# Two convolution layers in one kernel: the order of two half convolutions and a gelu in layer 0, and where layer 1's first pixel sums are kept

## The chip, the cores and the metric

The kernel runs on one core of one Trainium2 chip. A core has five engines that run side by side, each in its own program order: TensorE (PE in the profile, with PEld for the loads of its weights) multiplies matrices into PSUM; VectorE (DVE), ScalarE (ACT) and GpSimd (POOL) work on tiles; SyncE (SP) issues the DMAs between the main memory and the on-chip memory. They wait for each other by semaphores. The metric is the device time of one execution in microseconds (us), the median of several runs.

## The reference

The input x has 4 batches of 64 channels of 256 x 256 pixels, in fp32. Layer 0 and layer 1 each add their result to their input. Cut to what matters:

```python
# layer 0, on h0 = groupnorm(x)
h = gelu(conv3x3(h0, c1_w) + c1_b)               # 64 -> 64 channels
xa, k = split(conv1x1(h, c2_w))                  # 64 -> 128 channels, in halves
xs = gelu(taps_3x1(taps_1x3(xa)))                # depthwise, 3 taps across and 3 down
w = top2(softmax(mean(xs) @ gate_w.T))           # per batch: needs all of xs
out = xs + sum_i w_i * e_i_w3(e_i_w2(k) * e_i_w1(xs))   # three experts of rank 2, 4 and 8
x = x + proj(out)
# layer 1, on y = groupnorm(x)
h = relu(batchnorm(conv3x3(y, quantized(w1)) + b1))     # statistics over all batches
h = batchnorm(conv3x3(h, quantized(w2)) + b2)
x = x + relu(h + y)
```

## The kernel before

Two image rows lie on the 128 partitions at once (64 channels each). An *octet* is 8 rows of one batch, 32 to a batch; a *chunk* is 16 rows, 16 to a batch.

Layer 0 is worked octet by octet. Its 3x3 convolution takes two neighbouring pixels together by four products (0 to 3), whose inputs are sums and differences of pixels that POOL writes into v_ring (front_v, L492). Products 1 and 2 go into one PSUM bank (tag c, two buffers) by front_conv_a and front_conv_b with (1, 2). front_butterfly then brings them into the form in which products 0 and 3 can be added: ACT copies half (m, L558), DVE adds and subtracts (L559, L560). front_conv_a and front_conv_b with (0, 3) add the others, and front_h (two gelus on ACT, L566) empties the bank into h. The taps follow: front_taps_a and front_taps_b on PE (tag a, one buffer), front_taps_h with L615 on ACT, L616, L619 and L622 on DVE and the gelu L633 on ACT. front_k (L643), front_q (L681), front_proj (L653 on, with the DVE add L667) and the experts' out_slot (L754 on PE, L762 and two bn_stats L764 on DVE) share tag p, one buffer. divide sets a tick on POOL (L442) between two phases of PE: POOL's memset waits for the last matmul before it, and the first matmul of the next front_conv_b or front_taps_b waits for the memset.

The order is written out by hand: plan is a table from (step, order) to calls, and at(step, order, call) adds to it. Each octet takes one step in layer 0, so there are 128 steps, 32 to a batch. In step g, by order number: front_conv_a of octet g with (1, 2) at 1; out_slot of the batch before at 2; front_conv_a of octet g-1 with (0, 3) at 3; front_k, in one step of four, at 3.5; front_taps_a of octet g-3 at 4; divide at 5; front_proj of g-4 at 6; front_conv_b of g with (1, 2) at 7 and its butterfly at 7.5; front_conv_b of g-1 with (0, 3) at 8 and its gelu at 8.5; front_taps_b of g-3 at 9; front_q, in one step of four, at 10; front_taps_h at 11. The program order of PE, SP, DVE and POOL is that of the table; that of ACT too from step 124 on, and before that a scheduler sets it. Group norm's statistics of the next batch (L394 on DVE) are spread over the steps of batches 0 to 2. Experts of a batch run from step 36 on, one batch late: out_load and low_load (L738 and L744) fetch y and ranks, out_slot computes, and stores y_d<-y (L771) go out after each chunk.

At step 128 (CONV1) layer 1 begins; the tail of layer 0 is stretched to every second step (place). A chunk y_in is loaded (conv1_load, L788), normalized (conv1_affine, L793 on ACT) and split into a high and a low part (conv1_split: L354 on ACT, L356 on DVE and POOL). Sums of neighbouring pixels are made by add_pixels (L364 on POOL) and split as well (conv1_sums: L370 on ACT, L372 on POOL). conv1_a and conv1_b then work 8 rows (one d) in two steps: products into ps_h (tag c) and, from the sums, ps_hm (tag c while d < 4 in batch 0, then tag a). leave empties them: L335 on ACT writes m (tag ranks while d < 4 in batch 0), L336 on DVE writes h. In batch 0 the sums of the first four chunks were kept in tag t (one buffer, that of front_taps_h) and in tags xs or ranks. The last batch's experts run under layer 1, from step 164 on, a slot every 4.6 steps. conv2 works in the same manner, and a last pass adds everything up.

Of the kernel before, what the change touches and what calls it, by code (L numbers as in the profile page):

```python
# [9 lines left out]
F32 = mybir.dt.float32  # L10
# [7 lines left out]
B, C, H, W = 4, 64, 256, 256  # L18
P = 128
# [28 lines left out]
GF = GP * W  # L48
NG = NPAIR // GP
NOCT = NG // 2  # L50
CG = 4
CPAIR = CG * GP
# [11 lines left out]
def conv_preact_kernel(ctx: ExitStack, tc: tile.TileContext, io, col128, colset, col64):  # L64
# [30 lines left out]
    def flat(t):  # L95
        return t.rearrange("p a b -> p (a b)")
# [14 lines left out]
    def half_tile(pool, name, bufs, dtype=F32R):  # L111
        return pool.tile([P, CPAIR + 1, PW], dtype, tag="half", name=name, bufs=bufs)

    HW = W // 2
# [11 lines left out]
    def sum_tiles(pool, name, bufs):  # L126

        t = flat(half_tile(pool, f"sum_{name}", bufs))[:, 0 : 2 * (CPAIR + 1) * HW]
        t = t.rearrange("p (u a b) -> p u a b", u=2, b=HW)
        return [t[:, u] for u in range(2)]  # L130
# [4 lines left out]
    def split_tiles(pool, name):  # L135

        return [half_pads([half_tile(pool, f"half_{name}{i}{j}", 6) for j in range(2)]) for i in range(2)]
# [4 lines left out]
    work = layers.enter_context(tc.tile_pool(name="work", bufs=2))  # L142

    def chunk_out(name, tag, bufs):
        return work.tile([P, CPAIR, W], F32, tag=tag, name=name, bufs=bufs)
# [16 lines left out]
    def at(step, order, call, *args):  # L162
        plan[step, order].append((call, args))
# [181 lines left out]
    CUTS = (0, 5), (5, CPAIR + 1)  # L345

    def split(tiles, y, engines, cuts=CUTS):

        parts = []
        for a, e in cuts:  # L350
            upper, lower = (by_pixels(t, a, e) for t in tiles)
            parts.append((upper, lower, y[:, a:e, :].rearrange("p a (j e) -> p a e j", e=2)))
        for upper, _, y in parts:
            nc.scalar.activation(upper, y, AF.Copy)  # L354
        for (upper, lower, y), engine in zip(parts, engines):
            engine.tensor_tensor(lower, y, upper.bitcast(F32), ALU.subtract)  # L356

    def add_pixels(y, name, places, size):

        sums = []  # L360
        for (a, e), (pool, tag, bufs) in zip(CUTS, places):
            t = pool.tile(size, F32, tag=tag, name=f"s_{name}_{a}", bufs=bufs)
            t = (flat(t) if len(size) > 2 else t)[:, 0 : (e - a) * HW].rearrange("p (a b) -> p a b", b=HW)
            nc.gpsimd.tensor_tensor(t, y[:, a:e, 0::2], y[:, a:e, 1::2], ALU.add)  # L364
            sums.append(t)
        return sums

    def split_sums(tiles, sums):
        for (a, e), t in zip(CUTS, sums):
            nc.scalar.activation(tiles[0][:, a:e, :], t, AF.Copy)  # L370
        for (a, e), t in zip(CUTS, sums):
            nc.gpsimd.tensor_tensor(tiles[1][:, a:e, :], t, tiles[0][:, a:e, :].bitcast(F32), ALU.subtract)  # L372
# [403 lines left out]
    def out_end(b):  # L776
        gn2[b] = const.tile([P, 3], F32, name=f"gn2_{b}")
        yield from group_norm(st_y.pop(b), c128("avg4"), gn2[b][:, 0:2], f"y{b}")
        nc.vector.tensor_scalar(gn2[b][:, 2:3], gn2[b][:, 0:1], gn2[b][:, 1:2], -1.0, ALU.mult, ALU.mult)


    y_in, h_out, st_h = {}, {}, {}
# [16 lines left out]
    def conv1_split(b, k):  # L799

        split(halves[k % 2], y_in[b, k], (nc.vector, nc.vector if b == B - 1 else nc.gpsimd))

    sums_in = {}

    def conv1_add(b, k):
        sums_in[b, k] = add_pixels(y_in[b, k], f"1_{b}_{k}", [(work, "xs", 4)] * 2, [P, 2, GF])

    def conv1_prepare(b, k):

        places = (work, "t", 1), ((work, "ranks", 2) if k == 2 else (work, "xs", 4))  # L810
        sums_in[b, k] = add_pixels(y_in[b, k], f"1_{b}_{k}", places, [P, 2, GF])
        conv1_split(b, k)
        conv1_sums(b, k)

    def conv1_sums(b, k):
        del y_in[b, k]
        split_sums(sums[k % 2], sums_in.pop((b, k)))
# [75 lines left out]
    def at_each(places, chain):  # L893

        for place in places:
            at(*place, next, chain, None)
# [8 lines left out]
    def plan_front(b):  # L905
        t = b * F_STEPS
        place = tail if b == B - 1 else (lambda step: step)
        for k in range(NCH):
            if b > 0 or k >= 2:
                for call in (front_alloc, front_pad, front_load):  # L910
                    at(max(t + 2 * k - 3, 0), 0, call, b, k)
        for n in range(NOCT):
            g = t + n
            at(g, 1, front_conv_a, b, n, (1, 2))
            at(place(g + 1), 3, front_conv_a, b, n, (0, 3))
            at(place(g + 3), 4, front_taps_a, b, n)
            at(g, 5, divide)
            for step in (g + 1, g + 3):
                if step >= CONV1:
                    at(place(step), 5, divide)  # L920
            at(place(g + 4), 6, front_proj, b, n)
            at(g, 7, front_conv_b, b, n, (1, 2))
            at(g, 7.5, front_butterfly, b, n)
            at(place(g + 1), 8, front_conv_b, b, n, (0, 3))
            at(place(g + 1), 8.5, front_h, b, n)

            for half, before in ((1, 1), (0, 2)):
                if b > 0 or n > before - 1:
                    at(g - before, 5.4, front_v, b, n, half, ((1, 2),))
                    at(g - before, 9 if half else 9.5, front_v, b, n, half, ((0, 3),))  # L930
            at(place(g + 3), 9, front_taps_b, b, n)
            at(place(g + 3), 11, front_taps_h, b, n)
        for j in range(NOCT // 4):
            at(place(t + 4 * j + 5), 3.5, front_k, b, j)
            at(place(t + 4 * j + 7), 10, front_q, b, j)
        e = place(t + NOCT + 3)
        at_each(((e, 2.5), (e, 5.7), (e, 8.7)) if e < CONV1 else ((e + 1, 12.7), (e + 3, 12.7), (e + 5, 12.7)), gate(b))

# [12 lines left out]
    def plan_out(b, steps, order, end):  # L951

        for k in range(NCH):
            for call in (low_load, out_load):
                at(steps[2 * k - 3] if k > 1 else steps[0] - 2, order + 0.2, call, b, k)
            for i in range(2):
                at(steps[2 * k + i], order, out_slot, b, k, i)
        at_each(end, out_end(b))

    conv1_pool, halves, sums = [], [], []  # L960
# [13 lines left out]
    def plan_conv1(b):  # L974
        t = CONV1 + b * (NG + 1)
        if b == 0:
            at(t - 4, -1, conv1_first)
            at(t, 12, conv1_open)
        for k in range(NCH):
            load, affine, ready = t + 4 * k - 11, t + 4 * k - 6, t + 4 * k - 4  # L980
            if b == 0 and k < 4:

                load, affine, ready = ((t - 4, t - 3, t - 2), (t - 1, t, t + 2), (t + 1, t + 3, t + 4), (t + 5, t + 7, t + 8))[k]
            at(max(load, t + 6) if b == 0 and k > 3 else load, 0, conv1_load, b, k)
            at(affine, 5.6 if affine < t else 12.2, conv1_affine, b, k)
            if b == 0 and k < 4:

                at(ready, 5.6 if k < 2 else 13.1, conv1_prepare, b, k)
            else:
                at(affine, 12.3, conv1_add, b, k)  # L990
                at(ready, 13.1, conv1_split, b, k)
                at(ready, 13.2, conv1_sums, b, k)
        for d in range(NG // 2):
            at(t + 2 * d, 13, conv1_a, b, d)
            at(t + 2 * d + 1, 13, conv1_b, b, d)
        at(t + NG, 13, conv1_end, b)

    for b in range(B):
        plan_front(b)
        if b < B - 1:  # L1000
            plan_stats(b + 1, b * F_STEPS + 1, 2.7)
            t = (b + 1) * F_STEPS + 4
            e = t + NOCT + 1
            steps, end = [t + n for n in range(NOCT)], ((e, 5.5), (e + 1, 5.5), (e + 1, 9.95), (e + 2, 5.5))
# [5 lines left out]
        else:  # L1010
            t, e = CONV1 + 36, CONV1 + b * (NG + 1) - 10
# [25 lines left out]
    h_in = {}  # L1037
# [17 lines left out]
        split(halves2[i % 2], h_in[i], (nc.vector, nc.vector), cuts)  # L1055

    def conv2_add(i):
        sums_in[i] = add_pixels(h_in[i], f"2_{i}", [(halves_pool, "s", 2)] * 2, [P, 5 * HW])

    def conv2_sums(i):  # L1060
        del h_in[i]
# [10 lines left out]
    halves_pool = halves_stack.enter_context(tc.tile_pool(name="halves2", bufs=1, reuse_waits="tile"))  # L1072
    halves2 = split_tiles(halves_pool, "2")
    sums2 = [sum_tiles(halves_pool, f"2{i}", 6) for i in range(2)]
    h2, st_h2 = {}, {}

    def chunk_h2(b, k):
# [27 lines left out]
    with tc.manual_schedule(  # L1105
# [15 lines left out]
        for d in range(2 * len(chunks)):  # L1121
            i = d // 2
# [13 lines left out]
    steps = chunks[-KEEP:] + chunks[:-KEEP]  # L1136
# [21 lines left out]
    for i, (b, k) in enumerate(steps):  # L1158
        if i + AHEAD < len(steps):
            end_load(i + AHEAD)  # L1160
        y, h = y_of.pop(i), h2.pop((b, k))
# [7 lines left out]
        j = i - 3 + KEEP  # L1169
# [115 lines left out]
```

## Time and profile before

| what | us |
|---|---|
| median of 3 runs (lowest to highest) | 3377.47 (3375.42 to 3378.84) |
| the profiled execution, its own time | 3377.74 |
| its span, first to last instruction | 3376.0 |
| PE busy | 2683.1 (79%) |
| DVE busy | 2679.1 (79%) |
| ACT busy | 1658.2 (49%) |
| POOL busy | 1606.3 (48%) |

By stage (from the windows of the profile; us busy):

| stage | window | PE | DVE | ACT | POOL |
|---|---|---|---|---|---|
| start, statistics of batch 0 | 0 to 120 | 50.8 | 82.7 | 17.6 | 36.2 |
| layer 0, about one batch | 120 to 480 | 334.7 | 241.7 | 153.1 | 166.5 |
| layer 0, about one batch | 480 to 850 | 349.1 | 298.1 | 145.1 | 157.1 |
| layer 0, about one batch | 850 to 1220 | 348.6 | 295.0 | 146.7 | 156.3 |
| layer 0's last batch and the seam | 1220 to 1590 | 331.6 | 248.0 | 153.9 | 149.7 |
| layer 1, first convolution | 1590 to 2300 | 670.1 | 639.6 | 456.0 | 505.8 |
| layer 1, second convolution | 2300 to 2700 | 398.2 | 383.2 | 307.1 | 295.4 |
| end of it and last pass | 2700 to 3376 | 200.1 | 490.8 | 278.7 | 139.3 |

A stage whose PE column is close to the window's length is bound by PE. The profile's name for a line such as "PE ps_c L449 <- POOL v_ring L492" reads: PE stood idle before a matmul of line 449 into ps_c, and of the things that it waited for POOL's write of v_ring at line 492 was seen last. Matmul ends are modelled, so gaps of a tenth of a microsecond on PE mean nothing.

### The profile page before, as it was taken

How to read it: one execution, taken by the hardware profiler on the slowest of the kernel's cores; microseconds unless marked ns; L12 is line 12 of the kernel's file. 1: busy time of each engine (PE TensorE's matmuls, PEld its weight loads, DVE VectorE, ACT ScalarE, POOL GpSimd, SP SyncE). 2: the span in 40 equal slices, each digit the busy share in tenths (PEclk: the TensorE clock that was granted, in tenths of full speed). 3: DMA queues.
4: the chain of work that ended last, by engine and by line, in shares of the span. 5: the costliest groups of instructions: out<-in, count | busy, mean ns of one | idle time of the engine just before them, and what ended most of it. 6: DMA issues, size and time to landing. Idle time of an engine off the chain costs nothing.

```text
span 3376.0 us, 60519 instructions
## 1 busy us (share of the span) xinstructions
PE 2683.1 (79%) x24832; PEld 1772.7 (53%) x24832; DVE 2679.1 (79%) x2810; ACT 1658.2 (49%) x1799; POOL 1606.3 (48%) x1833
## 2 busy tenths in 40 slices
PE   2999999999999999997899999998999999300000
PEld 1555555554545555544667777776877878200000
DVE  7666588878888776665899998998999999866666
ACT  0344433343433343344666666667777777422222
POOL 2444543443444444443678777666777777100000
PEclk9999999999999999998999999999999999755555
DMA  8565588778886767674688987564666664599999
GB/s 305 161 174 137 143 263 270 229 218 251 268 267 191 206 196 218 197 216 144 219 291 283 303 298 246 218 252 173 238 238 238 238 232 171 202 412 412 412 412 387
DMA packets 356453, 838.27 MB, mean 248 GB/s; under 512 B 22288, under 2 KB 284944, under 8 KB 293456
## 3 DMA queue, kind: packets, MB, share of 16 engines
q1 hardware_dynamic: 356176, 834.40, 74.0%
q8 instruction: 195, 3.19, 0.4%
q14 instruction: 82, 0.67, 0.1%
HBM read 493.00 MB, written 341.31 MB: 247 GB/s over the span
## 4 chain that ended last, share of the span: by engine, by line
PE 58%; DVE 14%; DMA 12%; POOL 7%; issue 4%; ACT 4%; SPq 3%; POOLq 0%; ACTq 0%; DVEq 0%
PE ps_h L310 23%; PE ps_c L449 14%; DMA y_end<-y_d 10%; PE ps_a L449 7%; POOL v_ring L492 5%; PE ps_h2m L310 3%; PE ps_o L754 3%; PE ps_hm L310 2%; PE ps_p L449 2%; DVE half L356 2%; PE ps_k L643 2%; PE ps_q L681 2%; DVE h L336 2%; DVE y L762 1%; DVE t L619 1%
## 5 line engine op out<-in xcount | busy, mean ns | idle before, releaser
L310 PE MATMUL ps_h<-half,w_q 128*128 128x512 f32 x4096 | 1033.4, 404 | 23.4 <-DVE h L336 16.9
L310 PEld LDWEIGHTS ps_h<-half,w_q 128*128 128x128 f32 x4096 | 778.2, 191 | 253.0 <-issue 27.4
L372 POOL TENSOR_TENSOR sum<-s,sum 128x640 fp32r<-128x640 f32 (+1 forms) x256 | 556.8, 2196 | 195.0 <-ACT sum L370 189.3
L492 POOL TENSOR_TENSOR v_ring<-x 128x256 f32<-128x256 f32 x1024 | 593.3, 617 | 61.4 <-DMA x<-in_x 47.2
L449 PE MATMUL ps_c<-v_ring,u 64*64 64x256 f32 (+1 forms) x6472 | 391.3, 372 | 74.9 <-POOL v_ring L492 63.4
L449 PEld LDWEIGHTS ps_c<-v_ring,u 64*64 64x64 f32 x6472 | 273.6, 134 | 283.2 <-POOL v_ring L492 157.9
L442 POOL MEMSET tick<- 128x1 f32 x132 | 13.1, 99 | 820.1 <-PE ps_a L449 811.2
L336 DVE SCALAR_TENSOR_TENSOR h<-ps_h,scale_w,m 128x1024 f32<-128x1024 f32 x256 | 326.9, 1277 | 88.7 <-ACT m L335 88.7
L449 PE MATMUL ps_a<-h,av 64*64 64x512 f32 (+1 forms) x3568 | 386.3, 534 | 10.4 <-DVE t L619 9.1
L449 PE MATMUL ps_c<-v_ring,c1s 64*64 64x256 f32 (+1 forms) x6472 | 387.3, 368 | 0.5 <-DVE ps_c L560 0.5
L633 ACT ACTIVATE xs<-t 128x1024 f32<-128x1024 f32 x128 | 135.3, 1057 | 411.4 <-DVE t L622 375.9
L449 PEld LDWEIGHTS ps_c<-v_ring,c1s 64*64 64x64 f32 x6472 | 267.9, 133 | 129.0 <-DVE t L616 47.8
L1163 ACT ACTIVATE v<-y_end,shift,gn 128x2048 f32<-128x2048 f32 x64 | 133.8, 2092 | 321.2 <-DMA y_end<-y_d 314.4
L667 DVE TENSOR_TENSOR x<-ps_p,x 128x1024 f32<-128x1024 f32 x128 | 156.2, 1220 | 157.1 <-PE ps_p L449 131.5
L1164 DVE SCALAR_TENSOR_TENSOR h<-h,ss,v 128x2048 f32<-128x2048 f32 x64 | 150.2, 2351 | 160.3 <-DMA h<-h_d 103.4
L558 ACT ACTIVATE m<-ps_c 128x512 f32<-128x512 f32 x128 | 76.6, 598 | 378.3 <-PE ps_c L449 371.3
L356 DVE TENSOR_TENSOR half<-h,half 128x1280 fp32r<-128x1280 f32 (+1 forms) x128 | 254.4, 2029 | 7.7 <-ACT half L354 7.7
L616 DVE SCALAR_TENSOR_TENSOR t<-ps_a,m,t 128x1020 f32<-128x1020 f32 x128 | 163.5, 1277 | 122.2 <-ACT t L615 122.2
L449 PEld LDWEIGHTS ps_a<-h,av 64*64 64x64 f32 x3568 | 161.9, 133 | 148.5 <-issue 112.5
L356 DVE TENSOR_TENSOR half<-yn,half 128x1280 fp32r<-128x1280 f32 x80 | 211.3, 2658 | 4.2 <-ACT half L354 4.2
L335 ACT ACTIVATE m<-ps_hm,m,scale_w 128x512 f32<-128x512 f32 x128 | 99.6, 778 | 223.0 <-PE ps_hm L310 197.8
L566 ACT ACTIVATE h<-ps_c,c1b 128x512 f32<-128x512 f32 x256 | 172.2, 731 | 38.8 <-PE ps_c L449 38.8
(186 smaller groups left out, 4084.9 us busy)
## 6 DMA issues: line engine op xcount, KB each, us to landing
h_d<-h SPq DMA_DIRECT2D x117, 1024.0 KB, 4.8
h<-h_d SPq DMA_DIRECT2D x64, 1152.0 KB, 7.1
yn<-y_d SPq DMA_DIRECT2D x60, 1152.0 KB, 8.0
xs_in<-in_x SPq DMA_DIRECT2D x64, 1024.0 KB, 8.8
x<-in_x SPq DMA_DIRECT2D x256, 256.0 KB, 4.8
y<-t_d SPq DMA_DIRECT2D x64, 1024.0 KB, 8.7
y_d<-y SPq DMA_DIRECT2D x256, 256.0 KB, 5.1
y_end<-y_d SPq DMA_DIRECT2D x64, 1024.0 KB, 11.2
```

The source lines that it names most:

```text
L310: nc.tensor.matmul(ps[:, 0 : n * HW], w[:, k, m, :], t[:, i + m : i + m + n, c : c + HW], start=(j == 0), stop=(j == len(terms) - 1),)
L336: nc.vector.scalar_tensor_tensor(h.rearrange("p a (b e) -> p e (a b)", e=2), by_two(ps)[:, :, 0 : n * HW], w_scale[w], m.unsqueeze(1).to_b ...
L356: engine.tensor_tensor(lower, y, upper.bitcast(F32), ALU.subtract)
L372: nc.gpsimd.tensor_tensor(tiles[1][:, a:e, :], t, tiles[0][:, a:e, :].bitcast(F32), ALU.subtract)
L449: last[:] = [nc.tensor.matmul(ps[o, at_out[0] : at_out[1], :], w[i], rhs[i], **flags)]
L492: nc.gpsimd.tensor_tensor(v_of(p)[:, o : o + 2, :], *terms[p])
L566: nc.scalar.activation(h.rearrange("p q (c e) -> p e q c", e=2), c[:, t].rearrange("p (e q c) -> p e q c", e=2, q=GP), AF.Gelu, bias=c1_bi ...
L616: nc.vector.scalar_tensor_tensor(t[:, :, 1:W], ps[:, :, 0 : W - 1], sh[:, 0:1], t[:, :, 1:W], ALU.mult, ALU.add)
L633: nc.scalar.activation(flat(xss[b, n]), flat(t), AF.Gelu, accum_out=pooled[b][:, n : n + 1])
L667: nc.vector.tensor_tensor(t1, ps, t1, ALU.add)
L1163: nc.scalar.activation(v, y, AF.Identity, bias=shift[:, b : b + 1], scale=gn2[b][:, 1:2])
L1164: nc.vector.scalar_tensor_tensor(h, h, ss2[:, 0:1], v, ALU.mult, ALU.add)
```

## The change

Five edits. In layer 0's steps, front_conv_b with (0, 3) of octet g-1 and its gelu go from orders 8 and 8.5 to 6.6 and 6.8, so ahead of front_conv_b with (1, 2) of octet g and its butterfly; on ACT the two gelus L566 then stand ahead of the copy L558. In layer 1's start, the sums of the first four chunks go into a tile of tag o (three buffers, that of the experts' y), and the first chunk's adds, split and split of sums, which stood together at order 5.6 of step 126, go to order 9.7 of steps 125, 126 and 127. The last front_q goes from step 134 to 136. The experts' loads for chunk k are issued no earlier than four steps before their use: this leaves batches 0 and 1 and most of batch 2 as they are, moves chunks 14 and 15 of batch 2 from steps 125 and 127 to 138 and 146, and in the last batch moves the loads of chunks 2 to 15 from about 14 steps ahead to 4. In conv2 the sums go into two parts of one tile s2 and no longer into two buffers of a tag.

```diff
--- before.py
+++ after.py
@@ -355,15 +355,18 @@
         for (upper, lower, y), engine in zip(parts, engines):
             engine.tensor_tensor(lower, y, upper.bitcast(F32), ALU.subtract)
 
-    def add_pixels(y, name, places, size):
-
-        sums = []
-        for (a, e), (pool, tag, bufs) in zip(CUTS, places):
-            t = pool.tile(size, F32, tag=tag, name=f"s_{name}_{a}", bufs=bufs)
-            t = (flat(t) if len(size) > 2 else t)[:, 0 : (e - a) * HW].rearrange("p (a b) -> p a b", b=HW)
+    def add_pixels(y, places):
+
+        for (a, e), t in zip(CUTS, places):
             nc.gpsimd.tensor_tensor(t, y[:, a:e, 0::2], y[:, a:e, 1::2], ALU.add)
-            sums.append(t)
-        return sums
+        return places
+
+    def sum_places(name, pool, tag, bufs):
+
+        places = [pool.tile([P, 2, GF], F32, tag=tag, name=f"s_{name}_{i}", bufs=bufs) for i in range(2)]
+        return [
+            flat(t)[:, 0 : (e - a) * HW].rearrange("p (a b) -> p a b", b=HW) for (a, e), t in zip(CUTS, places)
+        ]
 
     def split_sums(tiles, sums):
         for (a, e), t in zip(CUTS, sums):
@@ -803,14 +806,12 @@
     sums_in = {}
 
     def conv1_add(b, k):
-        sums_in[b, k] = add_pixels(y_in[b, k], f"1_{b}_{k}", [(work, "xs", 4)] * 2, [P, 2, GF])
-
-    def conv1_prepare(b, k):
-
-        places = (work, "t", 1), ((work, "ranks", 2) if k == 2 else (work, "xs", 4))
-        sums_in[b, k] = add_pixels(y_in[b, k], f"1_{b}_{k}", places, [P, 2, GF])
-        conv1_split(b, k)
-        conv1_sums(b, k)
+        sums_in[b, k] = add_pixels(y_in[b, k], sum_places(f"1_{b}_{k}", work, "xs", 4))
+
+    def conv1_add_early(b, k):
+
+        t = flat(chunk_out(f"s_1_{b}_{k}", "o", 3))[:, 0 : (CPAIR + 1) * HW].rearrange("p (a b) -> p a b", b=HW)
+        sums_in[b, k] = add_pixels(y_in[b, k], [t[:, a:e, :] for a, e in CUTS])
 
     def conv1_sums(b, k):
         del y_in[b, k]
@@ -921,8 +922,8 @@
             at(place(g + 4), 6, front_proj, b, n)
             at(g, 7, front_conv_b, b, n, (1, 2))
             at(g, 7.5, front_butterfly, b, n)
-            at(place(g + 1), 8, front_conv_b, b, n, (0, 3))
-            at(place(g + 1), 8.5, front_h, b, n)
+            at(place(g + 1), 6.6, front_conv_b, b, n, (0, 3))
+            at(place(g + 1), 6.8, front_h, b, n)
 
             for half, before in ((1, 1), (0, 2)):
                 if b > 0 or n > before - 1:
@@ -930,9 +931,10 @@
                     at(g - before, 9 if half else 9.5, front_v, b, n, half, ((0, 3),))
             at(place(g + 3), 9, front_taps_b, b, n)
             at(place(g + 3), 11, front_taps_h, b, n)
+        e_last = b == B - 1
         for j in range(NOCT // 4):
             at(place(t + 4 * j + 5), 3.5, front_k, b, j)
-            at(place(t + 4 * j + 7), 10, front_q, b, j)
+            at(place(t + 4 * j + 7) + (2 if e_last and j == NOCT // 4 - 1 else 0), 10, front_q, b, j)
         e = place(t + NOCT + 3)
         at_each(((e, 2.5), (e, 5.7), (e, 8.7)) if e < CONV1 else ((e + 1, 12.7), (e + 3, 12.7), (e + 5, 12.7)), gate(b))
 
@@ -952,7 +954,7 @@
 
         for k in range(NCH):
             for call in (low_load, out_load):
-                at(steps[2 * k - 3] if k > 1 else steps[0] - 2, order + 0.2, call, b, k)
+                at(max(steps[2 * k - 3], steps[2 * k] - 4) if k > 1 else steps[0] - 2, order + 0.2, call, b, k)
             for i in range(2):
                 at(steps[2 * k + i], order, out_slot, b, k, i)
         at_each(end, out_end(b))
@@ -985,7 +987,10 @@
             at(affine, 5.6 if affine < t else 12.2, conv1_affine, b, k)
             if b == 0 and k < 4:
 
-                at(ready, 5.6 if k < 2 else 13.1, conv1_prepare, b, k)
+                add, parts, rest = ((t - 3, 9.7), (t - 2, 9.7), (t - 1, 9.7)) if k == 0 else [(ready, 5.6 if k == 1 else 13.1)] * 3
+                at(*add, conv1_add_early, b, k)
+                at(*parts, conv1_split, b, k)
+                at(*rest, conv1_sums, b, k)
             else:
                 at(affine, 12.3, conv1_add, b, k)
                 at(ready, 13.1, conv1_split, b, k)
@@ -1055,7 +1060,7 @@
         split(halves2[i % 2], h_in[i], (nc.vector, nc.vector), cuts)
 
     def conv2_add(i):
-        sums_in[i] = add_pixels(h_in[i], f"2_{i}", [(halves_pool, "s", 2)] * 2, [P, 5 * HW])
+        sums_in[i] = add_pixels(h_in[i], [s2[:, a:e, :] for a, e in CUTS])
 
     def conv2_sums(i):
         del h_in[i]
@@ -1072,6 +1077,7 @@
     halves_pool = halves_stack.enter_context(tc.tile_pool(name="halves2", bufs=1, reuse_waits="tile"))
     halves2 = split_tiles(halves_pool, "2")
     sums2 = [sum_tiles(halves_pool, f"2{i}", 6) for i in range(2)]
+    s2 = halves_pool.tile([P, CPAIR + 1, HW], F32, name="s2")
     h2, st_h2 = {}, {}
 
     def chunk_h2(b, k):
```

## The prediction

> **What bounds the kernel now.** In the page's slices PE is busy nine tenths or more almost everywhere up to the last sixth, so what counts is PE's gaps and what is late behind each. I read PE's waits stage by stage, then the timeline at each gap. Layer 0 has one gap that comes back (waits in the second batch's window: us in total, times, longest):
>
> ```profile
> PE ps_c L449 <- POOL v_ring L492: 16.1, 24, 0.8
> PE ps_k L643 <- DVE y L762: 1.3, 8, 0.2
> ```
>
> It names POOL. The chain of waits and the timeline at one such moment (start, us, what) name another:
>
> ```profile
> 618.47 0.62 POOL v_ring L492
> 619.09 0.39 issue
> 619.48 1.96 PE ps_c L449 x32
> ```
>
> ```profile
> 617.20 0.60 ACT L558 ACTIVATE m<-ps_c 128x512 f32<-128x512 f32 x1 [3.39 <-PE ps_c L449]
> 618.06 1.33 ACT L566 ACTIVATE h<-ps_c,c1b 128x512 f32<-128x512 f32 x2 [0.25 <-PE ps_c L449]
> 619.27 1.19 ACT L615 ACTIVATE t<-ps_a,tap_bias,m 128x1024 f32<-128x1024 f32 x1
> 619.48 1.96 PE L449 MATMUL ps_c<-v_ring,u 64*64 64x256 f32 x32 [0.67 <-POOL v_ring L492]
> 620.49 1.28 DVE L616 SCALAR_TENSOR_TENSOR t<-ps_a,m,t 128x1020 f32<-128x1020 f32 x1 [1.05 <-ACT t L615]
> 621.81 1.28 DVE L619 SCALAR_TENSOR_TENSOR t<-ps_a,m,t 128x1020 f32<-128x1020 f32 x1
> 623.21 1.28 DVE L762 SCALAR_TENSOR_TENSOR y<-ps_o,ob,y 128x1024 f32<-128x1024 f32 x1
> ```
>
> POOL was done 0.39 before PE went on, the gelu (L566, ends 619.39) 0.09; one step earlier the gaps are 0.44 and 0.10. The gelu empties the bank that PE wants, and starts 0.10 after products 0 and 3 end. The layers' seam holds the rest:
>
> ```profile
> 1519.77 3.38 PE L449 MATMUL ps_c<-v_ring,u 64*64 64x256 f32 x32 [3.53 <-POOL half L356]
> 1558.23 1.20 ACT L615 ACTIVATE t<-ps_a,tap_bias,m 128x1024 f32<-128x1024 f32 x1 [3.42 <-POOL sum L372]
> 1562.21 2.84 PE L449 MATMUL ps_a<-h,av 64*64 64x512 f32 x14 [4.11 <-DVE t L619]
> 1583.23 0.78 ACT L335 ACTIVATE m<-ps_hm,m,scale_w 128x512 f32<-128x512 f32 x1 [5.21 <-POOL sum L372]
> 1587.83 3.46 PE L681 MATMUL ps_q<-xs,m 128*32 128x512 f32 x16 [12.12 <-DVE x L667]
> ```
>
> Layer 1 under the last batch's experts is full on two engines (window: PE, PEld, DVE, ACT, POOL busy, then granted clock and DMA share):
>
> ```profile
> 1720.00:2070.00 350.00, 340.31 (x1395) 248.47 (x1394) 333.21 (x313) 230.43 (x227) 277.02 (x162) 0.99 0.87 294
> ```
>
> **What the Trainium skill says.** "PSUM — Partial Sum Buffer", section "Engine vs sequencer instructions": ScalarE, VectorE and GpSimd queues are strict FIFO. The trace agrees: L335's 5.21 us hold up everything behind it on ACT. "DMA: Bandwidth & Descriptors", section "Anatomy of one DMA — SWDGE (gpsimd) path": a semaphore wait happens on the issuing sequencer before dispatch. The trace agrees: four stores y_d<-y occupy SP from 1490.49 for 9.78 us, as they wait for DVE, and later loads stand behind them. "Perfetto Trace Analysis", section "Tensor Engine Instruction (MATMUL, LD_WEIGHTS)": PE's end times are estimates. So I take PE ends from when ACT starts (617.10, 617.96, hence 0.86 a half of conv_b, and 618.82 for taps_b).
>
> **Change 1: order in a step.** Nothing is added; DVE's and POOL's order stays. Call X the end of taps_b. Before, gelu ends at X+0.57 and PE waits 0.67. After, products 0 and 3 end at X-1.72, gelu runs X-1.62 to X-0.29: no wait. What is late next? m (L558) now follows gelu, ends near X+0.3; the butterfly (L559, L560, 0.70 each) ends near X+1.7; L615 follows m and ends near X+1.5; so L616 starts at X+1.7, where it started before (620.49 is X+1.67). The DVE chain from X is unmoved: L619 ends X+4.27, L762 X+5.67. PE after X: conv_a 1.96, experts' ps_o 1.06, conv_a 1.89, so taps_a could start at X+4.91. By kind of step:
> - Plain, with experts: taps_a needs L619, X+4.3, met. Gain 0.67.
> - Before front_k (one in four): ps_k needs the bank that L762 empties, X+5.7. Before, PE waited 0.67 and 0.16; after, 0.8 in one piece. Gain 0.
> - After front_q (one in four): its 1.85 hid gelu already. Gain 0.
> - First batch, no ps_o: taps_a started at 305.00, 0.15 after L619's end: bound by DVE already. Only the front_k step gains 0.67.
>
> Steps 36 to 125 have 45 plain ones: 45 x 0.67 = 30. The first 36 have 9 with front_k: 6. Sum -36. DVE must keep up: a plain step with three statistics holds 1.28+1.29+1.86+1.21+1.39+2.73 = 9.76 us of DVE in 10.07, so 0.3 is left. If DVE fails there (steps with statistics), half is lost: -18. If the first batch gains too: -42. I take -36.
>
> **Change 2: the seam** (times of the trace of before, so without what change 1 has moved). Step 125: the first chunk's two adds (2.24) go to POOL behind v_ring and wait for L793, which ends at 1503.4; behind them stands the tick of step 126, which waits for taps_a until 1512.97 anyway: 0. Step 126: POOL's sums no longer stand before gelu on ACT, but the two L354 (2.46) now stand before L615, so taps_a comes 1.4 late where conv_a came 3.53 late and taps_a followed unhindered: taps_a moves from 1525.92 to 1522.4, -3.5. Step 127's two L370 (1.25) hide behind front_q's 1.85. Second chunk: its sums no longer sit in tag t, so L615 starts at 1554.8 (end of L370), not 1558.23: -3.4. Third chunk: its sums leave ranks, so L335 follows L370 at 1578.0, not 1583.23. ps_h of d=3 needs that m: 1578.8 on; with its sum 5.1, to 1583.9; front_q, two steps later and behind it now, to 1585.8 (L667 is done by 1582.5); d=4 starts there, not at 1597.09: -11.3. Sum -18; ends -10 (the SP load of the fourth chunk, landing up to 13.5 after 1568.1, holds ACT up) and -22. The moved low_d<-k store has no reader before step 289. The sums take ring o, whose buffers are free since the last two experts' chunks of batch 2 load later. Chunk 14 of them stands on SP behind the low_d store, which waits for L685 (about 1588.9 by this count): ranks lands near 1595, and ps_o wants it at 1611.86 - 11.3 = 1600.6: 0.
>
> **Change 3: experts' loads four steps ahead.** For the last batch they were some 14 steps ahead. Now each stands on SP right behind the four stores of the chunk before, which wait for that chunk's second L762. Landing in this window: ranks 5.3/5.4/7.1, y 7.4/8.3/9.9 us (min, median, max). Chunk 8 as an example: stores leave SP at 1882.4, ranks lands 1887.9, PE wants it at 1885.43: 2.5 late; y, 1.2 behind, lands 1891.9, DVE wants it at 1888.87: 3.0. The same sum for chunks 2, 4, 6, 8, 10, 12, 14 gives PE 0.1+1.35+0.2+2.45+1.8+2.4+1.7 = 10.0. Odd chunks load y alone: DVE 0.1, 1.8, 1.5, 1.4 late, else nothing; these 4.8, and 3.4 by which y is later than ranks, fit in DVE's 350-333.2 = 16.8 idle. The last chunk of batch 2: DVE 1 late in a stretch full on DVE. I take +11; ends 0 (DVE, given rest, runs nearer to PE and the loads go earlier) and +25.
>
> **Rest.** s2 in conv2: the same adds with the same waits, POOL waits there for ACT (L372, 102 us in 2300 to 2700): 0; an added wait of 0.5 a chunk would be hidden by it. The step's tick now holds products 0 and 3 instead of 1 and 2: 0, front_proj's 0.86 covers it as before.
>
> Sum on the profiled execution: 3377.74 - 36 - 18 + 11 = 3334.7 (its span is 3376.0, 1.7 lie around it). The median of the runs is 0.3 lower: 3334.5.
>
> **Rivals.**
> - R1, DVE takes over: with statistics (0.3 us spare) and gate steps the DVE chain sets the step, three quarters of the 36 go. 3377.7-9-18+11 = 3362. For it: 9.76 of 10.07. Against: before L616 DVE still idled 1.05 in the old step.
> - R2, the late loads are hidden: 3377.7-36-18 = 3324. For it: DVE's slack. Against: PE itself waits for ranks.
> - R3, slower: the late loads decide. From 54/14 = 3.9 us lost per chunk on, all gain is eaten. With the slowest landings seen anywhere (ranks 8.8, y 13.5) the even chunks cost 34 and the odd 37, and batch 2 some 2: 3377.7-54+73 = 3397. For it: DMA share is 0.87 there. Against: those maxima are of other stages.
> - R4, it doesn't do what it says: PE really waits for POOL, as the page has it. Then only the seam gains: 3377.7-18+11 = 3371.
>
> **Numbers.** Forecast 0.60, R1 0.17, R2 0.15, R3 0.04, R4 0.04. The time is the forecast's, 3334.5. The forecast's unknowns together give about 3318 to 3352; R2 lies inside, R1 partly: 3315 to 3360. A run can tell 0.2%, 6.8 us, from none. Faster: forecast, R2, most of R1: 0.91. Same: a rest of R1 and half of R4: 0.04. Slower: R3 and a mishap: 0.05.
>
> **What would show it.** Right: the 0.7 us wait of ps_c gone from layer 0, a plain step 10.07 and four steps 44.9 instead of 46.3; ps_k waiting 0.8 for L762; d=4 starting some 50 us earlier than 1597; ps_o waiting 1 to 3 us for ranks in the last batch's experts. Wrong: DVE without idle before L616 and PE waiting for L619 or L560 in plain steps; ps_o waiting 5 us or more.

## The result, and the profile after

The changed kernel takes 3346.16 us (median of four runs, 3342.00 to 3350.72) where the kernel before takes 3376.44 beside it: a ratio of 0.991, 95% interval 0.9893 to 0.9927. The profiled execution took 3342.00, with a span of 3340.2. So it is 30 us faster, where 43 were forecast. (The profiled execution is the fastest of the four, so the comparison of traces below ends at 35.8.) One run of the kernel before, in the first set of experiments below, was slow (3443.92); without it that set's median is 0.2 lower.

The first answer is in layer 0. Of the waits in the window 480 to 850 of the changed kernel, with its columns as before, PE has no wait for v_ring left, and this in its place (line numbers above 364 are three higher than before: L569 is the gelu L566, L765 is L762):

```profile
PE ps_k L646 <- DVE y L765: 6.9, 8, 0.9
```

The timeline of one step before front_k, changed kernel (start, us, what):

```profile
578.97 1.05 PE L452 MATMUL ps_c<-v_ring,u 64*64 64x256 f32 x20
579.30 1.38 ACT L569 ACTIVATE h<-ps_c,c1b 128x512 f32<-128x512 f32 x2 [3.08 <-PE ps_c L452]
580.54 0.60 ACT L561 ACTIVATE m<-ps_c 128x512 f32<-128x512 f32 x1
580.78 1.96 PE L452 MATMUL ps_c<-v_ring,u 64*64 64x256 f32 x32
582.51 1.27 DVE L619 SCALAR_TENSOR_TENSOR t<-ps_a,m,t 128x1020 f32<-128x1020 f32 x1
583.82 1.28 DVE L622 SCALAR_TENSOR_TENSOR t<-ps_a,m,t 128x1020 f32<-128x1020 f32 x1
585.22 1.28 DVE L765 SCALAR_TENSOR_TENSOR y<-ps_o,ob,y 128x1024 f32<-128x1024 f32 x1
586.55 1.95 PE L646 MATMUL ps_k<-h,wk 64*32 64x512 f32 x32 [0.86 <-DVE y L765]
```

The gelu (L569) now ends at 580.68, and the next products start at 580.78 without a wait. Nothing on DVE has become earlier, so in this step the gap returns as 0.86 us before ps_k: L765 empties the bank that ps_k writes.

The layers' seam, changed kernel, with front_q (L684) behind the products of one more d:

```profile
1537.94 6.00 PE L310 MATMUL ps_h<-half,w_q 128*128 128x512 f32 x16 [3.03 <-ACT m L335]
1538.79 2.79 POOL L375 TENSOR_TENSOR sum<-s,sum 128x640 fp32r<-128x640 f32 x2
1544.80 1.92 PE L684 MATMUL ps_q<-xs,m 128*32 128x512 f32 x16
1544.91 0.78 ACT L335 ACTIVATE m<-ps_hm,m,scale_w 128x512 f32<-128x512 f32 x1 [4.83 <-PE ps_hm L310]
1546.66 2.16 PE L310 MATMUL ps_h<-half,w_q 128*128 128x512 f32 x8
```

ps_q's wait of 12.12 is gone. The L335 of d=2, which waited 5.21 for POOL, starts at 1537.09 without a wait; the one shown, of d=3, waits for PE. The products of d=4, which started at 1597.09, start at 1546.66, 50.4 earlier.

So far the changed kernel gains more than forecast. It loses under the last batch's experts. Waits in the window 1640 to 2040 of the changed kernel:

```profile
PE ps_o L757 <- DMA ranks<-low_d: 17.8, 7, 4.1
DVE y L765 <- DMA y<-t_d: 8.6, 4, 3.9
```

These seven are the even chunks 2 to 14, whose loads are moved; before, none of them waited (1.7 us went on chunk 0, whose load is not moved). The window that answers to the one before (PE, PEld, DVE, ACT, POOL busy) shows that neither engine is full any more:

```profile
1684.00:2033.00 349.00, 322.59 (x1310) 234.95 (x1309) 308.94 (x295) 213.83 (x210) 253.68 (x150) 0.98 0.81 278
```

From the start times of like instructions in both traces, before minus after:

| at | earlier by, us |
|---|---|
| octet 0, L670 | 4.9 |
| octet 119 | 35.5 |
| L336 of d=0, layer 1 | 38.0 |
| L336 of d=4 | 51.3 |
| L336 of d=8 | 56.1 |
| last chunk of the last experts, about 2050 | 34.5 |
| last instruction | 35.8 |

Up to d=8 some 56 us are won, and 21 of them are given back in the stretch where experts' loads stand four steps ahead.

### The profile page after: what moved, and what is told of

Its sections match the earlier page's. It is cut to its first block, busy times and chain, and to the rows that moved or that the text cites. A ratio compares the mean times of both kernels' runs of the same rounds, so it can differ in the third digit from the quotient of the medians.

```text
span 3340.2 us, 60547 instructions
## 1 busy us (share of the span) xinstructions
PE 2678.0 (80%) x24832; PEld 1767.8 (53%) x24832; DVE 2658.9 (80%) x2810; ACT 1647.6 (49%) x1799; POOL 1602.1 (48%) x1833
## 4 chain that ended last, share of the span: by engine, by line
PE 58%; DVE 18%; DMA 14%; ACT 5%; SPq 2%; issue 2%; POOL 1%; DVEq 0%; ACTq 0%; POOLq 0%
PE ps_h L310 23%; PE ps_c L452 12%; DMA y_end<-y_d 10%; PE ps_a L452 8%; PE ps_h2m L310 3%; PE ps_p L452 3%; PE ps_o L757 2%; DVE t L622 2%; DVE t L619 2%; PE ps_hm L310 2%; ACT h L569 2%; DVE h L336 2%; PE ps_k L646 2%; DVE y L765 2%; PE ps_q L684 2%
## 5 line engine op out<-in xcount | busy, mean ns | idle before, releaser
L310 PEld LDWEIGHTS ps_h<-half,w_q 128*128 128x128 f32 x4096 | 779.8, 192 | 251.9 <-issue 24.2
L375 POOL TENSOR_TENSOR sum<-s,sum 128x640 fp32r<-128x640 f32 (+1 forms) x256 | 555.5, 2190 | 199.2 <-ACT sum L373 193.6
L452 PE MATMUL ps_a<-h,av 64*64 64x512 f32 (+1 forms) x3568 | 385.5, 535 | 17.6 <-DVE t L622 17.6
L336 DVE SCALAR_TENSOR_TENSOR h<-ps_h,scale_w,m 128x1024 f32<-128x1024 f32 x256 | 326.8, 1277 | 84.7 <-ACT m L335 84.6
L452 PEld LDWEIGHTS ps_c<-v_ring,c1s 64*64 64x64 f32 x6472 | 253.5, 133 | 209.2 <-issue 97.9
L636 ACT ACTIVATE xs<-t 128x1024 f32<-128x1024 f32 x128 | 135.4, 1057 | 451.7 <-DVE t L625 410.7
L452 PEld LDWEIGHTS ps_c<-v_ring,u 64*64 64x64 f32 x6472 | 280.8, 134 | 135.0 <-POOL v_ring L495 77.9
L569 ACT ACTIVATE h<-ps_c,c1b 128x512 f32<-128x512 f32 x256 | 174.1, 740 | 345.4 <-PE ps_c L452 345.4
L670 DVE TENSOR_TENSOR x<-ps_p,x 128x1024 f32<-128x1024 f32 x128 | 156.2, 1220 | 144.1 <-PE ps_p L452 118.5
L356 DVE TENSOR_TENSOR half<-h,half 128x1280 fp32r<-128x1280 f32 (+1 forms) x128 | 254.3, 2028 | 7.7 <-ACT half L354 7.7
L562 DVE TENSOR_TENSOR ps_c<-m,ps_c 128x512 f32<-128x512 f32 x128 | 89.1, 696 | 177.6 <-ACT m L561 177.6
L335 ACT ACTIVATE m<-ps_hm,m,scale_w 128x512 f32<-128x512 f32 x128 | 99.6, 778 | 240.8 <-PE ps_hm L310 220.6
L356 DVE TENSOR_TENSOR half<-yn,half 128x1280 fp32r<-128x1280 f32 x80 | 202.5, 2548 | 4.2 <-ACT half L354 4.2
L356 POOL TENSOR_TENSOR half<-yn,half 128x1024 fp32r<-128x1024 f32 x48 | 118.5, 2469 | 138.7 <-ACT half L354 138.7
```

The source lines that it names most:

```text
L310: nc.tensor.matmul(ps[:, 0 : n * HW], w[:, k, m, :], t[:, i + m : i + m + n, c : c + HW], start=(j == 0), stop=(j == len(terms) - 1),)
L335: nc.scalar.activation(m, by_two(ps_m)[:, 0, 0 : n * HW], AF.Identity, bias=bias, scale=w_scale[w])
L336: nc.vector.scalar_tensor_tensor(h.rearrange("p a (b e) -> p e (a b)", e=2), by_two(ps)[:, :, 0 : n * HW], w_scale[w], m.unsqueeze(1).to_b ...
L452: last[:] = [nc.tensor.matmul(ps[o, at_out[0] : at_out[1], :], w[i], rhs[i], **flags)]
L569: nc.scalar.activation(h.rearrange("p q (c e) -> p e q c", e=2), c[:, t].rearrange("p (e q c) -> p e q c", e=2, q=GP), AF.Gelu, bias=c1_bi ...
L636: nc.scalar.activation(flat(xss[b, n]), flat(t), AF.Gelu, accum_out=pooled[b][:, n : n + 1])
```

## The experiments

Eleven more kernels, each measured beside the kernel before, whose median was 3377.4 to 3378.5 in these sets. "Gain" is the difference of the medians of one set.

| run | median, us | gain | ratio, 95% interval |
|---|---|---|---|
| order in a step alone | 3343.37 | 34.9 | 0.9895 (0.9879 to 0.9911) |
| late loads alone | 3402.45 | -24.2 | 1.0071 (1.0056 to 1.0087) |
| change without late loads | 3319.95 | 58.3 | 0.9829 (0.9813 to 0.9844) |
| seam alone | 3354.76 | 23.5 | 0.9929 (0.9911 to 0.9946) |
| loads six steps ahead | 3318.29 | 59.9 | 0.9823 (0.9809 to 0.9838) |
| ranks six, y four steps ahead | 3324.44 | 52.9 | 0.9842 (0.9827 to 0.9856) |
| front_k earlier | 3324.31 | 53.9 | 0.9844 (0.9829 to 0.9859) |
| seam, sums in old places | 3357.46 | 20.8 | 0.9941 (0.9926 to 0.9956) |
| seam, first chunk in one step | 3358.37 | 19.9 | 0.9941 (0.9924 to 0.9957) |
| seam, front_q in old place | 3366.82 | 10.6 | 0.9968 (0.9955 to 0.9980) |
| front_q moved alone | 3368.18 | 10.4 | 0.9968 (0.9958 to 0.9979) |

### The three parts apart

**Order in a step alone**, on the kernel before:

```diff
-            at(place(g + 1), 8, front_conv_b, b, n, (0, 3))
-            at(place(g + 1), 8.5, front_h, b, n)
+            at(place(g + 1), 6.6, front_conv_b, b, n, (0, 3))
+            at(place(g + 1), 6.8, front_h, b, n)
```

> The kernel before with only the order of layer 0's steps changed (products 0 and 3 and their gelu ahead of the other octet's products 1 and 2). My theory: PE's 0.7 us wait was for the gelu, so this alone brings what the changed kernel has at octet 119, some 35 us: about 3341. The rival, that PE waited for POOL's v_ring as the page names it, gives no change: 3377. If the order gains only together with the other edits: in between.

It gained 34.9, and POOL's order and work are untouched. Nor does the new order only let POOL finish earlier: of the eight v_ring writes of a step, the sixth, which the chain named before (618.47 to 619.09), runs here from 580.48 to 581.09, and PE goes on at 580.73, before its end. So the theory that PE waits for POOL falls: the view of waits named the wrong one of two semaphores.

**Late loads alone**, on the kernel before:

```diff
-                at(steps[2 * k - 3] if k > 1 else steps[0] - 2, order + 0.2, call, b, k)
+                at((max(steps[2 * k - 3], steps[2 * k] - 4) if b == B - 1 else steps[2 * k - 3]) if k > 1 else steps[0] - 2, order + 0.2, call, b, k)
```

> The kernel before with only the last batch's experts' loads put off to four steps ahead of their use. Theory: PE then waits for ranks and DVE for y, and 20 us are lost, as the changed kernel's lead over the one before falls from 56 to 35 us in that stretch: about 3397. My forecast's own count was +11: 3388. Rival, that the lead is lost for another reason (the earlier layer 1 collides with something): 3377.

It lost 24.2, with PE waiting 17.6 us in eight waits for ranks (1.7 of it for chunk 0, as before). The forecast's 11 is too small by more than half, and most of the cost doesn't depend on the seam or on layer 0.

**The change without late loads**, on the changed kernel:

```diff
-                at(max(steps[2 * k - 3], steps[2 * k] - 4) if k > 1 else steps[0] - 2, order + 0.2, call, b, k)
+                at(max(steps[2 * k - 3], steps[2 * k] - (99 if b == B - 1 else 4)) if k > 1 else steps[0] - 2, order + 0.2, call, b, k)
```

> The changed kernel with the last batch's loads as far ahead as before; the two late chunks of batch 2 stay late. Theory: the 20 us come back, about 3325, and the runs lie closer together than the changed kernel's 3342 to 3351, since no wait for a landing is left on the path. Rival: 3346, the lead is lost all the same.

It gained 58.3, so the late loads cost the changed kernel 3346.16 - 3319.95 = 26.2 by medians and 3340.2 - 3316.8 = 23.4 by spans. The waits for ranks are gone.

**The seam alone** (this one, with orders 8 and 8.5 again; the late loads of batch 2's chunks 14 and 15 and conv2's s2 are still in it):

> As e3_loads_ahead, but with layer 0's steps in the order of before: only the edits at the seam are left. Theory: they bring what the traces show between octet 120 and the eighth d of layer 1, 20 us (forecast 18), less the 0.7 us that step 126 would have anyway: about 3357. Rival, that a later wait takes the seam's gain back (the gate's DVE chain): 3377.

It gained 23.5, by the profiled spans 20.7. And 34.9 + 23.5 = 58.4, the 58.3 of both together: order and seam don't disturb each other.

### The late loads

The forecast placed the ranks of a chunk by a rule: right behind the stores of the chunk before, plus some 5.5 us. For chunk 8, its example, the changed kernel does just that:

```profile
1827.34 4.96 SPq L774 DMA_DIRECT2D y_d<-y  x4
1832.40 1.20 SPq L747 DMA_DIRECT2D ranks<-low_d  x1
1838.01 1.13 PE L757 MATMUL ps_o<-ranks,wm 32*128 32x512 f32 x4 [2.68 <-DMA ranks<-low_d]
```

Ranks lands 5.5 after its issue, and PE waits 2.68 where 2.45 was forecast. Chunk 10 is different:

```profile
1875.15 9.63 SPq L774 DMA_DIRECT2D y_d<-y  x4
1885.21 0.81 SPq L855 DMA_DIRECT2D h_d<-h  x1
1886.12 1.44 SPq L747 DMA_DIRECT2D ranks<-low_d  x1
1893.43 1.65 PE L757 MATMUL ps_o<-ranks,wm 32*128 32x512 f32 x4 [4.14 <-DMA ranks<-low_d]
```

The stores hold SP for 9.63 us and leave it at 1884.78. Then an h_d store, which the count left out, stands ahead of ranks, so that ranks is issued 1.3 later. And it lands 7.3 after its issue, not 5.5: PE waits 4.14 where 1.8 was forecast. The seven chunks, in us:

| chunk | 2 | 4 | 6 | 8 | 10 | 12 | 14 |
|---|---|---|---|---|---|---|---|
| PE's wait, forecast | 0.1 | 1.35 | 0.2 | 2.45 | 1.8 | 2.4 | 1.7 |
| PE's wait, changed kernel | 0.84 | 2.67 | 0.74 | 2.68 | 4.14 | 2.96 | 3.77 |
| issue of ranks to landing | 5.8 | 6.7 | 5.7 | 5.5 | 7.3 | 5.3 | 7.2 |

Chunks 4, 10 and 14, which have an h_d store ahead of ranks, make 5.7 of the 7.8 us that the forecast is short. The table of DMA issues (KB each, median us to landing), first of the kernel before (window 1720 to 2070), then of the changed one (1684 to 2033):

```profile
ranks<-low_d SPq DMA_DIRECT2D x6, 512.0 KB, 5.5
```

```profile
ranks<-low_d SPq DMA_DIRECT2D x6, 512.0 KB, 6.2
```

The landing time used in the forecast was that of loads some 14 steps ahead, in the kernel before. Six steps ahead of their use, the loads stand ahead of the stores of the chunk before:

```diff
-                at(max(steps[2 * k - 3], steps[2 * k] - 4) if k > 1 else steps[0] - 2, order + 0.2, call, b, k)
+                at(max(steps[2 * k - 3], steps[2 * k] - (6 if b == B - 1 else 4)) if k > 1 else steps[0] - 2, order + 0.2, call, b, k)
```

> The changed kernel with the last batch's loads six steps ahead of their use (four in the changed kernel, about 14 before). Theory: the loads were late because they stand on SP behind the stores of the chunk before, which wait for DVE; six steps is ahead of those stores, so all of the 26 us that e3_loads_ahead won (3319.95) come back but for a microsecond or two: 3320 to 3324. Rival, that distance alone counts and a landing under this load needs more than 16 us: about 3330 or more.

3318.29, with no wait for ranks or y: the cost is all in the place behind the stores, and the rival falls. (A landing there takes a median of 7.2 us for ranks, which nobody waits for.) With only ranks six steps ahead (`6 if b == B - 1 and call is low_load else 4`):

> The changed kernel with the last batch's loads of ranks six steps ahead of their chunk, and its loads of y four steps ahead as the change has them. All loads six ahead gave 3318.3, all four ahead 3346.2: 28 between them. Theory, the one the prediction counted with: PE's waits for ranks are what is lost (17.8 us in seven of them), and a late y fits into DVE's idle: 3318 to 3324, no wait of ps_o for ranks, the waits of DVE for y still there. Rival: y lands late as well and decides next, since PE waits for the banks that DVE empties: 3332 to 3346, with ps_o or ps_k waiting for L765 in place of ranks.

3324.44, just above the theory's range and well below the rival's. Late ranks are 3346.16 - 3324.44 = 21.7 of the cost, late y 3324.44 - 3319.95 = 4.5; the runs of this kernel lie 8.6 apart, so the parts are good to a few us. The 21.7 is more than the 17.8 of waits. Behind three of them PE's granted clock is low for a while in the changed kernel: 0.68 (1838.00 to 1841.50), 0.57 (1893.43 to 1897.00) and 0.68 (2001.90 to 2005.40), and 1.00 behind the one of chunk 12 (1946.20 to 1949.70). An estimate from these figures, each stretch times what its clock lacks of 1, is another 3.8 us. This kernel's waits, window 1640 to 2060:

```profile
DVE y L765 <- DMA y<-t_d: 10.0, 6, 2.7
PE ps_h L310 <- DVE h L336: 14.0, 8, 4.3
```

There is no wait for ranks, and DVE's waits for y are no smaller than with all loads late. The second line is 9.1 us in six waits with the loads as before: 4.9 more, as DVE comes late to L336. So the prediction's reading seems to hold for half of it: DVE's idle time takes up about half of y's 10 us, not all.

### The step before front_k

The 0.86 before ps_k is left in one step of four. On the change without late loads, front_k goes ahead of the experts' out_slot, so that ps_k takes a bank already emptied:

```diff
-            at(place(t + 4 * j + 5), 3.5, front_k, b, j)
+            at(place(t + 4 * j + 5), 1.5, front_k, b, j)
-            at(t + int(g / per), 3.5, stats_group, b, g)
+            at(t + int(g / per), 3.1 if (t + int(g / per)) % 4 == 1 else 3.5, stats_group, b, g)
-                at(steps[2 * k + i], order, out_slot, b, k, i)
+                at(steps[2 * k + i], 3.2 if order == 2 and steps[2 * k + i] % 4 == 1 and steps[2 * k + i] < CONV1 else order, out_slot, b, k, i)
```

> As e3_loads_ahead, and in the steps with front_k its products are put right behind the first conv_a and the experts' slot behind the second, with the statistics ahead of it on DVE. Theory: these steps gained nothing from the new order since ps_k waits 0.9 us for the bank that L762 empties at the end of the DVE chain; with the bank free at that place 23 waits of 0.9 go, 17 to 20 us: 3300 to 3303. Rival, that the wait only moves (ps_o waits for ACT's L651, or front_proj for L762): 3320. Second rival, DVE is the bound there and idles before L762: slower than 3320.

3324.31 against 3319.95: nothing gained, rather a little lost. The timeline of that kernel:

```profile
580.88 1.95 PE L646 MATMUL ps_k<-h,wk 64*32 64x512 f32 x32
583.61 1.06 ACT L636 ACTIVATE xs<-t 128x1024 f32<-128x1024 f32 x1 [3.16 <-DVE t L625]
584.67 1.09 ACT L654 ACTIVATE k<-ps_k,k_bias 128x1024 f32<-128x1024 f32 x1
585.82 1.13 PE L757 MATMUL ps_o<-ranks,wm 32*128 32x512 f32 x4 [1.10 <-ACT k L654]
```

ps_k is done near 582.8 without a wait. But L654, which empties its bank, stands on ACT behind the gelu L636, and that waits 3.16 us for DVE. The next user of the bank, ps_o, waits 1.10 for it, 8.8 us in eight waits in the window 480 to 850, where ps_k waited 6.9. So the wait has moved, as the first rival says. In layer 0 a scheduler sets ACT's order; L654 ahead of L636 wasn't tried.

### The seam's parts

The first three are the seam alone with one part undone. **Sums of chunks 1 to 3 (counted from 0) back in the tags t, xs and ranks** (the diff is cut to where they go):

```diff
+        if k:
+            places = (("t", 1), (("ranks", 2) if k == 2 else ("xs", 4)))
```

> As e4_seam_only (3354.76), but the sums of the second to fourth chunk are kept in tags t, xs and ranks as before; the first stays in ring o. Theory: L615 again waits 3.4 us for POOL's read of t, and L335 5.2 us for its read of ranks: +8.7, about 3363.5. Rival, that front_q's later place and the three steps hold the whole gain: 3355.

It gave back 2.7 of the 8.7 expected, 3.7 by the profiled spans; the intervals of the two ratios overlap. Its timeline has the old wait of tag t:

```profile
1554.96 1.20 ACT L618 ACTIVATE t<-ps_a,tap_bias,m 128x1024 f32<-128x1024 f32 x1 [3.47 <-POOL sum L375]
1574.66 0.76 ACT L335 ACTIVATE m<-ps_hm,m,scale_w 128x512 f32<-128x512 f32 x1
1575.45 1.28 DVE L336 SCALAR_TENSOR_TENSOR h<-ps_h,scale_w,m 128x1024 f32<-128x1024 f32 x1 [0.48 <-ACT m L335]
```

The 3.47 is back and costs 2.5 at d=2 (L336 at 1575.45, not 1572.95) and 3.2 at d=3 (1583.95, not 1580.71). L335 shows no wait for POOL behind ranks: the 5.21 is missing. This doesn't show that the old place in ranks was harmless, since the run leaves another condition of that wait away. Tag ranks has two buffers. In the kernel before, and in the last experiment below, the ranks of batch 2's chunk 14 are loaded near 1500.4 and hold one of them through the seam, so that the sums and m share the other. In all kernels with the seam's edits this load comes later, here at 1588.69, and both buffers are free. By this reading either edit alone, the sums' new place or the later load, takes L335's wait away; no run tests the two apart.

**First chunk's add, split and sums in one step again**, at order 5.6 of step 126:

```diff
-                add, parts, rest = ((t - 3, 9.7), (t - 2, 9.7), (t - 1, 9.7)) if k == 0 else [(ready, 5.6 if k == 1 else 13.1)] * 3
+                add, parts, rest = [(ready, 5.6 if k < 2 else 13.1)] * 3
```

> As e4_seam_only (3354.76), but add, split and sums of the first chunk stand together in step 126 at order 5.6 again. Theory: gelu and the copy m wait again behind the sums on ACT, 3.5 us on PE where now taps_a waits: +3.5, about 3358. Rival: the wait is taken up by the seam's later waits, 3355.

```profile
1519.87 3.55 PE L452 MATMUL ps_c<-v_ring,u 64*64 64x256 f32 x32 [3.52 <-POOL half L356]
```

The wait is back as it was, and the median is 3.6 higher. In the seam L336 of d=0 is 3.2 later than in the seam alone (1550.62, not 1547.38): the 3.52, and 1.6 by which the 32 products behind the wait take longer (3.55 us; in the seam alone 1.96), less waits of 1.19 and 0.69 that go for it. At d=5 it is 3.7 later. But the intervals of the two ratios overlap and the profiled spans differ by 0.9 only, so how much of it is left at the end, between 1 and 3.6 us, these runs don't tell.

**front_q in its old place**, step 134:

```diff
-            at(place(t + 4 * j + 7) + (2 if e_last and j == NOCT // 4 - 1 else 0), 10, front_q, b, j)
+            at(place(t + 4 * j + 7), 10, front_q, b, j)
```

> The seam alone (orders in a step and last batch's loads as before), with front_q of the last batch's last four octets back two steps, in step 134, where the kernel before has it. The experiment with the seam alone gave 3354.8 (-23.5), and giving the sums of chunks 2 to 4 their old places back cost only 2.7 of it. Theory: the move of front_q is a part of the gain by itself, since in its old place ps_q waits for L667 and L335's sum while PE has nothing else: 3358.5 (-20), with a wait of ps_q of 3 to 5 us. Rival: once ring o has taken the sums the move brings nothing: 3355. Second rival: the move is the larger part, and ps_q waits 10 us or more again as before: 3365.

12 of the seam's 23.5 go with it: the second rival, though with a ps_q wait of 6.8, not 10. The start times of L336 show two steps, not one. Against the seam alone it is late by 1.3 from d=0 on, ahead of front_q's place (one group of 20 products takes 3.61 us in this execution, not 1.95), by 6.8 at d=3 (1587.46, not 1580.71) and by 10.9 at d=5. So the move itself makes 5.4 and then 9.6. The second loss is on DVE. The gate's last part there, and POOL beside it, in this kernel:

```profile
1598.23 2.25 POOL L361 TENSOR_TENSOR s<-yn 128x640 f32<-128x640 f32 x2 [1.98 <-ACT yn L796]
1598.68 0.17 DVE L714 RECIPROCAL tot<-tot 128x1 f32<-128x1 f32 x1
1601.18 2.42 POOL L356 TENSOR_TENSOR half<-yn,half 128x1024 fp32r<-128x1024 f32 x1 [0.70 <-ACT half L354]
1601.28 2.34 DVE L724 TENSOR_TENSOR keep<-gate,keep 128x3 f32<-128x3 f32 x1
1603.56 2.76 POOL L375 TENSOR_TENSOR sum<-s,sum 128x640 fp32r<-128x640 f32 x2
1603.65 1.47 DVE L728 TENSOR_TENSOR pick<-keep,m 128x12 f32<-128x12 f32 x1
1605.43 1.17 DVE L733 TENSOR_TENSOR wm<-row,pw 128x256 f32<-128x256 f32 x1
1606.59 1.27 DVE L336 SCALAR_TENSOR_TENSOR h<-ps_h,scale_w,m 128x1024 f32<-128x1024 f32 x1
1607.92 6.02 PE L310 MATMUL ps_h<-half,w_q 128*128 128x512 f32 x16 [4.55 <-DVE h L336]
```

and two of these in the seam alone (POOL has no work from 1593.8 to 1595.7 there):

```profile
1594.60 0.16 DVE L724 TENSOR_TENSOR keep<-gate,keep 128x3 f32<-128x3 f32 x1
1595.27 0.42 DVE L733 TENSOR_TENSOR wm<-row,pw 128x256 f32<-128x256 f32 x1
```

Three elements a partition take 2.34 us instead of 0.16, up to the end of POOL's L356. From L713 to the end of L737 the gate takes 8.2 us instead of 3.9, L336 stands behind it, and PE waits 4.55 for L336. The kernel before has the same 2.34 and the same 4.55.

**front_q moved alone**, on the kernel before (the same line, the other way):

> The kernel before with one edit: the last batch's front_q goes from step 134 to step 136. With everything else of the seam it gave 3354.8 instead of 3366.8, so 12.0. Theory: the move works by itself, since PE takes d=4's products while it would wait for L667, and the experts' gate on DVE then falls into a stretch in which POOL is idle: 3377.5 - 12 = 3365.5, with the gate's last part on DVE (L713 to L737) taking some 4 us instead of 8, and the wait of ps_h for L336 of 4.6 after it gone. Rival: with the third chunk's sums still in ranks, L335 waits its 5.2 us for POOL all the same and d=4 with it: 3372 to 3375. Second rival: the old places of the sums cost nothing once front_q is moved, and the move alone is worth what the whole seam without the three steps is, some 17 to 20: 3358 to 3361.

It gained 10.4: the theory's 12, nearly, and between the two rivals. Its timeline (line numbers of the kernel before):

```profile
1583.61 0.78 ACT L335 ACTIVATE m<-ps_hm,m,scale_w 128x512 f32<-128x512 f32 x1 [5.22 <-POOL sum L372]
1584.44 5.83 PE L310 MATMUL ps_h<-half,w_q 128*128 128x512 f32 x16 [8.36 <-ACT m L335]
1605.94 0.16 DVE L721 TENSOR_TENSOR keep<-gate,keep 128x3 f32<-128x3 f32 x1
```

L335 still waits 5.22 for POOL, and PE 8.36 for it, where it waited 12.12 for ps_q before. L336 of d=3 is 5.0 earlier (1592.05, not 1597.07); the gate, 3.9 instead of 8.2, brings 4.2 more by d=5 (1607.03, not 1616.21). So the move wins by two mechanisms of about equal size, and only the first has to do with PE's order.

## Why the prediction was right, and where it was wrong

The time, 3334.5, was 12 us too low, inside its range; the direction was right. By its steps:

- **Change 1, -36**: measured alone, -34.9. Its mechanism holds line by line: PE waited for the gelu, ps_k now waits 0.86 (0.8 forecast), and the first batch is held by DVE (PE's waits for L622 there are 12.0 us in 22, longest 0.6). The parts differ. Four steps with experts take 44.6 us, not 44.9, and a plain one 9.90, not 10.07: a gain of 0.83, which fits the 0.67 and the 0.16 that the count named for the front_k step only. The first octet is 4.9 earlier, which no term had, since a table load of 1.28 for the first gelu and two waits of the filling pipeline no longer stand on PE's path, nor the 1.75 by which 64 products behind the longer wait (2.60) took longer (2.81 and 2.86 us, not 1.96 each). One to two us come back at each change of batch. These happen to cancel.
- **Change 2, -18**: measured alone, -23.5, by spans -20.7. There d=4 starts at 1581.65, 15.4 earlier than 1597.09, where the three terms make 18. The last of them gives 15.4 less the 5.8 by which L336 of d=1 is earlier, 9.6 of its 11.3; tag t 2.7 of 3.4 (3.2 at d=3); the first chunk 1 to 3.6 of 3.5. The third term puts L335's wait down to the sums in ranks alone and leaves out the buffer that the later load of chunk 14 sets free. Missing too was the gate: 4.2 more by d=5, since it falls into a stretch in which POOL mostly idles.
- **Change 3, +11**: this is the step that failed, by size. It measures +24.2 alone and +26.2 in the changed kernel. "PE 10.0" is 17.8 us of waits and costs 21.7, the rest mostly since PE's granted clock is low behind three of them (by the estimate above). The term takes 5.3 to 5.5 us for a landing that takes 5.3 to 5.8 in four chunks and 6.7 to 7.3 in three, and in these three it sets ranks right behind the stores where an h_d store lets it out 1.3 to 1.7 behind their end. And "these 4.8 ... and 3.4 ... fit in DVE's idle" holds for about half: late y costs 4.5. The range's upper end of +25 for this term was nearly reached.
- **Rest, 0**: the lead is 34.5 us at the last batch's last chunk and 35.8 at the end, so conv2 and the last pass together changed by some 1.3 us (s2 was not measured by itself).
- **Rivals**: R1 (DVE takes over) falls: 34.9 of 36 came. R2 (late loads hidden) falls: 26 us. R3's mechanism is what happened, at half of the 54 from which it decides. R4 falls by the order alone.

That the time lies inside the range owes something to luck: changes 2 and 3 both moved more than forecast, and the 3 to 5.5 us more of change 2 hide a part of what change 3 was short by.

The term of change 3 was sized from the landing times of loads that nobody waited for. It also is the only part that makes the kernel slower: with the loads six steps ahead the kernel takes 3318.29, and beats both (0.9823 of the kernel before, interval 0.9809 to 0.9838).

## What to carry to other kernels

The lead of a load is counted from the last DMA ahead of it on the same queue that waits for a semaphore: two steps more, ahead of a store that waits for DVE, were worth 28 us here, and nothing else changed. Where a wait hangs on two semaphores, look in the timeline which writer ended just before the start; the view of waits named POOL where the gelu on ACT ended 0.09 before. And a gap of PE closed in one place is won only if what is late next, here the bank that L765 empties, isn't late by as much. Last, two edits that each remove a wait hide each other when only one of them is undone: the missing 5.21 above is such a case, by the reading given there.

## What the runs showed of the hardware

DVE operations with two inputs in SBUF were held up while POOL worked: L724, three elements a partition, took 0.16 us with POOL idle and 2.34 beside L356 on POOL, up to its end, while L714, with one input, took 0.17 beside L361 on POOL. The big DVE L356 took 1.48 us alone and 3.60 beside POOL's L356 and L375. The Trainium skill, "SBUF — State Buffer", section "Who interferes with whom", says so: a DVE instruction with two SBUF inputs contends with a GpSimd instruction that reads SBUF. The traces agree, and add that it decides a place in a schedule: 4.2 us of the seam came from moving the gate to where POOL idles.

TensorE ran at about half its clock for a while behind some of its waits, so such a wait cost more than its own length. In the kernel before the granted clock was 0.50 from 1519.77 to 1521.50, behind the wait of 3.53, and 1.00 from 1506.00 to 1508.00, behind one of 0.67; the same 32 products took 3.38 and 1.96 us. Behind the 12.12 it was 0.50 (1587.83 to 1591.00). How long a wait must be isn't settled by these runs: behind the same wait of 2.14 it was 0.50 with front_q in its old place (1533.88 to 1537.00) and 1.00 in the seam alone (1534.20 to 1536.10), and behind one of 2.96 in the changed kernel 1.00 (1946.20 to 1949.70).
